# Experts of a Mamba and mixture-of-experts layer: every expert on every row, or each expert on rows sorted for it

## The chip, the cores and the metric

The kernel runs on one core of a Trainium2 chip. The metric is the device time of one execution in microseconds. The engines of the core are TensorE (PE in the profile, its weight loads PEld), VectorE (DVE), ScalarE (ACT), GpSimd (POOL) and SyncE (SP); each works through its own instructions in order and waits for the others by semaphores. SP issues most of the DMAs here.

## The reference

The input is 32 sequences of 512 tokens with 256 features, in fp32. In short form, each sequence goes through one Mamba block with an MLP, then through a mixture of experts, with layer norms between:

```python
# first part, per sequence
h = x + mamba(layernorm(x))           # inner width 512, 16 states, scan over 512 tokens
y = h + gelu(layernorm(h) @ w1.T + b1) @ w2.T + b2
x = layernorm(x + y)
# second part: 8 experts of inner width 128, two for each token, and a shared one
scores = softmax(xf @ gate_w.T)
_, idx = top_k(scores, 2)
cw = zeros(N, 8); cw[row, idx] += scores at idx
g = einsum('nd,efd->nef', xf, wg); u = einsum('nd,efd->nef', xf, wu)
y = einsum('nef,edf->ned', silu(g) * u, wd)
routed = einsum('ned,ne->nd', y, cw)
shared = silu(xf @ sg.T) * (xf @ su.T) @ sd.T
x = layernorm(x + routed + shared)
```

As written, the reference computes all eight experts for every token and multiplies six of the eight results by zero.

## The kernel before

The kernel keeps 128 channels or 128 tokens on the partitions. A sequence has four parts. `front` normalizes the tokens, projects them, applies the convolution and the gates of the time step, and stores two tables, `sdt` and `sdx`, to DRAM. `scan` runs the recurrence in 32 steps per sequence: SP loads `dtr` and `dxr` from those tables (the list `dtr<-sdt` and `dxr<-sdx`, line 322, three buffers each, two chunks of two steps ahead), `times_b` multiplies by the B table (line 357, on POOL for a quarter of the steps, else on DVE), ACT writes the decay to PSUM (line 418), DVE runs the scan instruction (line 420), POOL multiplies by the C table (line 421), and PE sums the states into `py` (line 385) two steps later. The tile `u` that goes through these steps has eight buffers. `middle` projects out, adds and runs the MLP. `back` normalizes, computes the gate's logits, routes, and runs the experts.

The parts of different sequences overlap. While `scan(b)` runs, the generator `finish(b - 1)` is advanced a unit at a time between its steps: middle of b - 1, front of b + 1, back of b - 1. The emitted order is then placed on the engines by the framework's scheduler, and each engine follows its list in order.

In `back` (lines 573 to 596) nine rounds run, for the shared expert and the eight routed ones. In each, PE computes `pg` and `pu` for the 512 tokens (line 189), ACT the tanh of the gate (line 584), DVE two operations (lines 591 and 592), PE the down projection `pd` in four pieces of 128 tokens (line 196), and DVE adds each piece to the sum `h`, scaled by the token's weight `cwt` for that expert (line 567), which is zero for six of eight. `route` (lines 482 to 524) works on small tiles of 128 x 32, mostly in PSUM. All expert weights lie in SBUF (`wg_sb`, `wu_sb`, `wd_sb`). POOL issues no DMA.

## Time and profile before

| | |
|---|---|
| median of three runs | 5848.29 us (5845.99 to 5848.46) |
| profiled execution | 5845.93 us |
| its span, first to last instruction | 5843.9 us |
| TensorE clock granted | 0.917 of full speed |
| busy: DVE, PE, POOL, ACT | 4950.2, 4875.3, 3649.2, 2965.3 us |
| DMA | 447.93 MB, mean 77 GB/s; queue of SP 22.6% of the 16 engines |

A busy time is what the instructions of one engine took together; it says nothing about what they waited for. The profile has for that the chain that ended last (from the last instruction back, each step to what released it) and, with each group of instructions, the idle time of its engine just before it and the engine that ended it. A group is one line of the code with one operation and one pair of tiles. The matmuls of fp32 appear as two passes each.

### The profile page before, as it was taken

To read this page: it belongs to the slowest core of one execution; us is meant where nothing else is said; L and a number is where in the kernel's file an instruction comes from. 1 tells how busy PE (TensorE), PEld (TensorE's weight loads), DVE (VectorE), ACT (ScalarE), POOL (GpSimd) and SP (SyncE) were. 2 spreads that over 40 slices of the span, in tenths; PEclk is the share of its full clock that TensorE was granted. 3 is DMA by queue.
4 is the path that set the end of the run, shared out by engine and by line. 5 is a ranking of instruction groups with operands and counts; after the bars stand their busy time and mean duration, and the time that the engine had idled before them with its cause. 6 is when DMAs were issued, how large, how long until landed. Compare 5 with 4: busy or idle time off the path is not lost.

```text
span 5843.9 us, 47922 instructions
## 1 busy us (share of the span) xinstructions
PE 4875.3 (83%) x14336; PEld 2073.3 (35%) x14336; DVE 4950.2 (85%) x7303; ACT 2965.3 (51%) x4512; POOL 3649.2 (62%) x2127
## 2 busy tenths in 40 slices
PE   5688888888888888888888888888888888888887
PEld 1233333333333333333333333333333333333343
DVE  6888888888889888888888888888888888888885
ACT  4544555445555445554455544455544555444542
POOL 5766666665666656666666656566666666665652
PEclk7899999999989999899998999999999999999998
DMA  4222222222221222222222212222222222222210
GB/s 149 74 78 76 75 84 75 70 83 80 73 84 64 83 78 76 82 69 78 81 73 81 85 63 82 78 72 87 69 76 76 75 84 79 68 82 80 73 58 13
DMA packets 239701, 447.93 MB, mean 77 GB/s; under 512 B 23104, under 2 KB 57024, under 8 KB 239312
## 3 DMA queue, kind: packets, MB, share of 16 engines
q1 hardware_dynamic: 236448, 439.49, 22.6%
q10 hardware_dynamic: 2992, 5.38, 0.3%
q8 instruction: 112, 1.84, 0.1%
q14 instruction: 149, 1.22, 0.1%
HBM read 358.81 MB, written 85.98 MB: 76 GB/s over the span
## 4 chain that ended last, share of the span: by engine, by line
DVE 42%; PE 36%; POOL 9%; ACT 7%; issue 4%; DMA 0%; ACTq 0%; DVEq 0%; POOLq 0%
DVE u L420 21%; PE py L385 11%; DVE u L357 6%; PE pg L189 6%; PE pd L196 6%; POOL u L421 5%; PE pu L189 4%; DVE pin L244 4%; DVE h L567 2%; PE pm L189 2%; PE pm L196 2%; ACT pda L418 2%; POOL dt L295 2%; PE pz L189 1%; POOL dtx L297 1%
## 5 line engine op out<-in xcount | busy, mean ns | idle before, releaser
L421 POOL TENSOR_TENSOR u<-u,bc 128x1024 f32<-128x1024 f32 x1024 | 2410.5, 2356 | 1778.4 <-DVE u L420 1691.1
L420 DVE TENSOR_TENSOR_SCAN u<-pda,u 128x512 f32<-128x512 f32 x2048 | 2439.5, 1211 | 121.4 <-ACT pda L418 117.3
L418 ACT ACTIVATE pda<-dtr,a_neg 128x512 f32<-128x512 f32 x2048 | 1396.7, 689 | 1338.0 <-DVE u L420 1333.3
L385 PE MATMUL py<-u,gather 128*32 128x512 f32 x4096 | 1389.1, 664 | 442.0 <-POOL u L421 393.9
L357 DVE TENSOR_TENSOR u<-dx,bc 128x1024 f32<-128x1024 f32 x768 | 923.6, 1210 | 83.2 <-ACT dx L354 78.1
L385 PEld LDWEIGHTS py<-u,gather 128*32 128x32 f32 x4096 | 238.5, 115 | 1249.6 <-POOL u L421 606.5
L189 PE MATMUL pg<-x1T,wg_sb 128*128 128x512 f32 x1152 | 634.6, 653 | 30.7 <-DVE the L591 28.1
L196 PE MATMUL pd<-wd_sb,he 128*128 128x256 f32 x2304 | 613.7, 386 | 24.6 <-DVE h L567 24.3
L357 POOL TENSOR_TENSOR u<-dxr,bc 128x1024 f32<-128x1024 f32 x256 | 602.4, 2353 | 4.8 <-PE py L385 2.8
L196 PEld LDWEIGHTS pd<-wd_sb,he 128*128 128x128 f32 x2304 | 421.0, 189 | 403.9 <-DVE h L567 168.0
L189 PE MATMUL pu<-x1T,wu_sb 128*128 128x512 f32 x1152 | 551.2, 596 | 1.3
L584 ACT ACTIVATE the<-pg 128x512 f32<-128x512 f32 x288 | 171.9, 597 | 662.9 <-PE pg L189 662.9
L567 DVE SCALAR_TENSOR_TENSOR h<-pd,cwt,h 128x256 f32<-128x256 f32 x1024 | 450.0, 480 | 55.6 <-PE pd L196 51.3
L196 PE MATMUL po<-out_sb,xc 128*128 128x256 f32 x1024 | 303.0, 452 | 53.8 <-DVE h L440 28.6
L189 PEld LDWEIGHTS pg<-x1T,wg_sb 128*128 128x128 f32 x1152 | 215.6, 206 | 281.7 <-issue 90.4
L189 PEld LDWEIGHTS pu<-x1T,wu_sb 128*128 128x128 f32 x1152 | 219.6, 193 | 269.0 <-issue 230.8
L189 PE MATMUL pin<-xnT,in_sb 128*128 128x512 f32 x512 | 252.0, 625 | 52.9 <-DVE xc L256 49.8
L244 DVE SCALAR_TENSOR_TENSOR pin<-xpad,half,pin 128x512 f32<-128x512 f32 x384 | 269.8, 748 | 22.4 <-POOL dtx L297 12.0
L196 PEld LDWEIGHTS po<-out_sb,xc 128*128 128x128 f32 x1024 | 223.8, 228 | 174.3 <-DVE xc L403 63.0
L262 PE MATMUL pdbc<-xc,xp_sb 128*48 128x512 f32 x256 | 175.0, 846 | 131.9 <-DVE xc L256 131.8
L591 DVE SCALAR_TENSOR_TENSOR the<-the,pg 128x512 f32<-128x512 f32 x288 | 195.8, 680 | 99.9 <-ACT the L584 99.9
L189 PE MATMUL pm<-hT,w_sb 128*128 128x512 f32 x512 | 239.3, 611 | 43.2 <-ACT hT L451 22.6
(107 smaller groups left out, 5030.0 us busy)
## 6 DMA issues: line engine op xcount, KB each, us to landing
dtr<-sdt SPq DMA_DIRECT2D x512, 256.0 KB, 2.9
dxr<-sdx SPq DMA_DIRECT2D x512, 256.0 KB, 3.0
bc<-rows SPq DMA_DIRECT2D x128, 512.0 KB, 4.5
sdt<-dt SPq DMA_DIRECT2D x64, 512.0 KB, 2.8
sdx<-dtx SPq DMA_DIRECT2D x64, 512.0 KB, 3.0
x<-in_x_dram SPq DMA_DIRECT2D x32, 512.0 KB, 3.8
out_dram<-h SPq DMA_DIRECT2D x32, 512.0 KB, 5.4
rows<-dbc SPq DMA_DIRECT2D x32, 64.0 KB, 1.6
```

Source lines behind the costliest of these rows:

```text
L189: nc.tensor.matmul(p, w[:, k, cols], src[:, k, :], start=(k == 0), stop=(k == KM - 1))
L196: nc.tensor.matmul(p, part[:, c * P : (c + 1) * P], w[:, j, :], start=(j == 0), stop=(j == len(parts) - 1),)
L244: nc.vector.scalar_tensor_tensor(pa, xp[:, i : i + S], half[:, w0 + i : w0 + i + 1], pa, ALU.mult, ALU.add,)
L262: nc.tensor.matmul(pd[: R + 2 * NS, :], xp_sb[:, j, :], xcs[j], start=(j == 0), stop=(j == NJ - 1),)
L357: eng.tensor_tensor(u, dx.unsqueeze(1).to_broadcast([P, GS, S]), table(0, b, g), ALU.mult)
L385: nc.tensor.matmul(py[r : r + ND, :], gather, u[:, i, :], start=False, stop=(g == NH - 1 and i == GS - 1),)
L418: nc.scalar.activation(pda, dtr, AF.Exp, scale=a_neg[:, a : a + 1])
L420: nc.vector.tensor_tensor_scan(ui, pda, ui, 0.0, ALU.mult, ALU.add)
L421: nc.gpsimd.tensor_tensor(u, u, table(1, b, g), ALU.mult)
L567: nc.vector.scalar_tensor_tensor(a, p, cw[:, c, e : e + 1], a, ALU.mult, ALU.add)
L584: nc.scalar.activation(th, pg, AF.Tanh, scale=0.5)
L591: nc.vector.scalar_tensor_tensor(th, th, 1.0, pg, ALU.add, ALU.mult)
```

## The change

Each token's row is now computed only by the two experts that it chose. The 32 sequences form groups: six of four, then four of two. For each sequence, `route` finds the two experts of each token and also, with matmuls against a triangular matrix (`before`) and ones, the token's place among the tokens of that expert in the group. `back` runs only the shared expert, and writes each token's row twice, with eight indirect DMAs from POOL, into the DRAM table `rows_in` at those places (2048 places per expert, two tables used in turn, set to zero by `clear` while sequences 0 and 1 are finished). The sum of input and shared expert goes to DRAM as `sums`.

When a group is complete, `experts(g)` computes from the counts a list of blocks of 128 rows of one expert. Their number isn't known when the program is built; it runs the worst case, 39 blocks for a group of four and 23 for a group of two. For each block SP reads two numbers from SBUF into registers and loads the block's rows and its expert's weights (a row of 768 numbers per partition) from DRAM; two blocks at a time go through transposes, gate and up projection, tanh and products, down projection, and a store to `rows_out`. At the end POOL fetches, with an indirect DMA for each 128 tokens and choice, the two result rows of each token; PE sums them, each multiplied by a diagonal matrix of the tokens' weights, and the final layer norm follows. This work is spread as a second generator, `late`, over the steps of the scans that follow.

Besides, `xpad` and `thz` have one buffer instead of two, and `dt` and `dtx` are computed in two halves. The diff, without the changes of shapes and names around it:

```diff
+    before = const.tile([P, P], F32, name="before")
+    nc.gpsimd.iota(
+        before, [[1, P]], base=0, channel_multiplier=-1, allow_small_or_imprecise_dtypes=True
+    )
+    nc.vector.tensor_scalar(before, before, 0.0, 1.0, ALU.is_gt, ALU.mult)
+    ones = const.tile([P, P], F32, name="ones")
+    nc.gpsimd.memset(ones, 1.0)
+    first = const.tile([P, E], F32, name="first")
+    for e in range(E):
+        nc.gpsimd.memset(first[:, e : e + 1], float(e * CAP))
...
-            xp = work.tile([P, NTAP - 1 + S], F32, tag="xpad", name=f"xpad_{b}_{j}")
+            xp = work.tile([P, NTAP - 1 + S], F32, tag="xpad", name=f"xpad_{b}_{j}", bufs=1)
-            th = work.tile([P, S], F32, tag="thz", name=f"thz_{b}_{j}")
+            th = work.tile([P, S], F32, tag="thz", name=f"thz_{b}_{j}", bufs=1)
...
+            dt = work.tile([P, 2, S], F32, tag="dt", name=f"dt_{b}_{j0}", bufs=1)
+            dtx = work.tile([P, 2, S], F32, tag="dtx", name=f"dtx_{b}_{j0}", bufs=1)
+            for i, j in enumerate(range(j0, j0 + 2)):
+                pa = ps.tile([P, S], F32, tag="tk", name=f"pdt_{b}_{j}")
+                nc.tensor.matmul(
+                    pa, dt_sb[:, j * P : (j + 1) * P], dbc[:R, :], start=True, stop=True
+                )
+                yield
+                nc.scalar.activation(dt[:, i, :], pa, AF.Abs, bias=col("dtb", j))
+                nc.vector.tensor_scalar(
+                    dtx[:, i, :], pa, col("dtb", j), 0.0, ALU.add, ALU.max
+                )
+            nc.scalar.activation(dt, dt, AF.Exp, scale=-1.0)
+            nc.scalar.activation(dt, dt, AF.Ln, bias=1.0)
...
+    rows_in = [scr.tile([E * CAP + P, DM], F32, name=f"rows_in{i}", bufs=1) for i in range(2)]
+    carries, slots, weights = {}, {}, {}
+
+    def clear(t):
+
+        z = work.tile([P, GS, S], F32, tag="u", name=f"zero_{t}", bufs=U_BUFS)
+        nc.gpsimd.memset(z, 0.0)
...
+        r = rows_in[t]
+        nc.sync.dma_start(
+            r[: full * P].rearrange("(m p r) d -> p m (r d)", p=P, r=n),
+            z.unsqueeze(1).to_broadcast([P, full // n, n * DM]),
+        )
...
+        nc.tensor.matmul(pos, before, both, start=True, stop=False)
+        for c in range(NC - 1):
+            k = NC - 1 - c
+            nc.tensor.matmul(
+                pos[:, c + 1 :, :],
+                ones,
+                both[:, c : c + 1, :].to_broadcast([P, k, E]),
+                start=False,
+                stop=(c == NC - 2),
+            )
+        for c in range(NC):
+            nc.tensor.matmul(tot, ones, both[:, c, :], start=(c == 0), stop=(c == NC - 1))
...
+        carry = tl("carry", [P, E])
+        nc.vector.tensor_tensor(carry, carries[g], tot, ALU.add)
+        carries[g] = carry
+        nc.vector.tensor_tensor(tmp, one, pos, ALU.mult)
+        nc.vector.tensor_reduce(slot[:, 0, :], tmp, AX.X, ALU.add)
+        nc.vector.tensor_tensor(tmp, both, pos, ALU.mult)
+        nc.vector.tensor_reduce(s2, tmp, AX.X, ALU.add)
+        nc.vector.tensor_tensor(slot[:, 1, :], s2, slot[:, 0, :], ALU.subtract)
+        idx = tl("idx", [P, TOPK * NC], I32)
+        nc.vector.tensor_copy(idx, slot.rearrange("p k c -> p (k c)"))
...
-        for e in [E, *range(E), None]:
-            if e is not None:
-                pg = ps.tile([P, S], F32, tag="mm", name=f"pg_{b}_{e}")
-                pu = ps.tile([P, S], F32, tag="mm", name=f"pu_{b}_{e}")
-                channels(pg, wg_sb[:, :, e, :], slice(0, P), x1T)
-                channels(pu, wu_sb[:, :, e, :], slice(0, P), x1T)
...
+        wg, wu, wd = parts(ws_sb)
+        channels(pg, wg, slice(0, P), x1T)
+        channels(pu, wu, slice(0, P), x1T)
+        yield
+        th = work.tile([P, S], F32, tag="th", name=f"th_{b}", bufs=1)
+        nc.scalar.activation(th, pg, AF.Tanh, scale=0.5)
+        t = work.tile([P, S], F32, tag="hid", name=f"he_{b}", bufs=HID_BUFS)
+        nc.vector.scalar_tensor_tensor(th, th, 1.0, pg, ALU.add, ALU.mult)
+        nc.vector.scalar_tensor_tensor(t, pu, 0.5, th, ALU.mult, ALU.mult)
+        r = rows_in[place[b][0] % 2]
+        for k in range(TOPK):
+            for c in range(NC):
+                i = k * NC + c
+                nc.gpsimd.indirect_dma_start(
+                    out=r,
+                    out_offset=bass.IndirectOffsetOnAxis(ap=idx[:, i : i + 1], axis=0),
+                    in_=h[:, c, :],
+                    in_offset=None,
+                    bounds_check=E * CAP + P - 1,
+                    oob_is_err=True,
+                )
+                yield
...
+            v = h[:, c0 : c0 + 2, :]
+            nc.vector.tensor_tensor(v, v, po, ALU.add)
+        sums[b] = scr.tile([P, NC, DM], F32, tag="sums", name=f"sums_{b}", bufs=3 * GROUP)
+        nc.sync.dma_start(sums[b], h)
+
+    def experts(g):
+
+        nb = n_blocks(g)
...
+        cnt, num, cum = [tl(nm, [P, E]) for nm in ("cnt", "num", "cum")]
+        nc.vector.tensor_tensor(cnt, carries.pop(g), first, ALU.subtract)
+        m = TOPK * len(groups[g]) * S // P
+        cmp = tl("cmp", [P, E * MAX_BLOCKS])
+        a = cmp[:, : E * m].rearrange("p (e m) -> p e m", m=m)
+        nc.vector.tensor_tensor(
+            a,
+            cnt.unsqueeze(2).to_broadcast([P, E, m]),
+            mults[:, :m].unsqueeze(1).to_broadcast([P, E, m]),
+            ALU.is_gt,
+        )
+        nc.vector.tensor_reduce(num, a, AX.X, ALU.add)
+        nc.vector.tensor_tensor_scan(cum, ones[:, :E], num, 0.0, ALU.mult, ALU.add)
...
+        row, wrow = [tl(nm, [P, nb], I32) for nm in ("row", "wrow")]
+        nc.vector.tensor_scalar(row, st, float(E * CAP), 1.0, ALU.min, ALU.mult)
+        nc.vector.tensor_scalar(wrow, ex, float(P), 1.0, ALU.mult, ALU.mult)
...
+        got = small.tile([P, n], I32, tag="got", name=f"got_{g}", bufs=2)
+        nc.vector.tensor_tensor(got, back_to, flat, ALU.add)
...
+        def fetch(k):
+            got = []
+            for i in range(2 * k, min(2 * k + 2, nb)):
+                r = in_order(row[0:1, i : i + 1], E * CAP)
+                x = work.tile([P, DM], F32, tag="xb", name=f"xb_{g}_{i}", bufs=4)
+                nc.sync.dma_start(x, rows_in[g % 2][bass.ds(r, P), :])
+                r = in_order(wrow[0:1, i : i + 1], E * P)
+                w = work.tile([P, NW], F32, tag="wb", name=f"wb_{g}_{i}", bufs=4)
+                nc.sync.dma_start(w, w_e[bass.ds(r, P), :])
+                got.append((x, w))
+            return got
+
+        pairs = (nb + 1) // 2
+        ahead = fetch(0)
+        for k in range(pairs):
+            pair = ahead
+            ahead = fetch(k + 1) if k + 1 < pairs else None
+            n = len(pair)
+            pt = ps.tile([P, KM, 2, P], F32, tag="tk", name=f"pt_{g}_{k}")
+            for i, (x, _) in enumerate(pair):
+                for q in range(KM):
+                    nc.tensor.transpose(pt[:, q, i, :], x[:, q * P : (q + 1) * P], ident)
...
+            xT = work.tile([P, KM, 2, P], F32, tag="xT", name=f"xT_{g}_{k}")
+            nc.scalar.copy(xT[:, :, :n, :], pt[:, :, :n, :])
...
+            pm = ps.tile([P, 2, 2, P], F32, tag="mm", name=f"pe_{g}_{k}")
+            for i, (_, w) in enumerate(pair):
+                for a, v in enumerate(parts(w)[:2]):
+                    for q in range(KM):
+                        nc.tensor.matmul(
+                            pm[:, a, i, :],
+                            v[:, q, :],
+                            xT[:, q, i, :],
+                            start=(q == 0),
+                            stop=(q == KM - 1),
+                        )
...
+            nc.scalar.activation(th_, pg, AF.Tanh, scale=0.5)
+            nc.vector.scalar_tensor_tensor(th_, th_, 1.0, pg, ALU.add, ALU.mult)
+            nc.vector.scalar_tensor_tensor(he_, pu, 0.5, th_, ALU.mult, ALU.mult)
...
+            po = ps.tile([P, 2, DM], F32, tag="tk", name=f"pd_{g}_{k}")
+            for i, (_, w) in enumerate(pair):
+                nc.tensor.matmul(
+                    po[:, i, :], he[:, i, :], parts(w)[2], start=True, stop=True
+                )
+            yb = work.tile([P, 2, DM], F32, tag="yb", name=f"yb_{g}_{k}")
+            nc.scalar.copy(yb[:, :n], po[:, :n])
+            nc.sync.dma_start(
+                rows_out[2 * k : 2 * k + n].rearrange("i p d -> p i d"), yb[:, :n]
+            )
+            yield
...
+        for i0, b in enumerate(groups[g]):
+            at = work.tile([P, NC, DM], F32, tag="at", name=f"at_{b}", bufs=1)
+            nc.sync.dma_start(at, sums.pop(b))
+            for c0 in range(0, NC, 2):
+                po = ps.tile([P, 2, DM], F32, tag="tk", name=f"pc_{b}_{c0}")
+                for c in range(c0, c0 + 2):
+                    for k in range(TOPK):
+                        i = (i0 * TOPK + k) * NC + c
+                        y = work.tile([P, DM], F32, tag="yg", name=f"yg_{b}_{k}_{c}", bufs=4)
+                        nc.gpsimd.indirect_dma_start(
+                            out=y,
+                            out_offset=None,
+                            in_=src,
+                            in_offset=bass.IndirectOffsetOnAxis(
+                                ap=got[:, i : i + 1], axis=0
+                            ),
+                            bounds_check=nb * P - 1,
+                            oob_is_err=True,
+                        )
+                        dg = work.tile([P, P], F32, tag="dg", name=f"dg_{b}_{k}_{c}", bufs=2)
+                        nc.scalar.mul(dg, ident, weights[g][:, i0, k, c : c + 1])
+                        nc.tensor.matmul(
+                            po[:, c - c0, :],
+                            dg,
+                            y,
+                            start=(k == 0),
+                            stop=(k == TOPK - 1),
+                        )
+                    yield
+                v = at[:, c0 : c0 + 2, :]
+                nc.vector.tensor_tensor(v, v, po, ALU.add)
...
+        end = min(groups[g][-1] + 2, NB) if g < len(groups) else NB
+        now = -(-n_late // max(end - b, 1))
...
+            while lately * (per - 1) < i * now and n_late:
+                next(late, None)
+                lately += 1
+                n_late -= 1
...
+        if g < len(groups) and b == groups[g][-1] + 1:
+            run(late)
+            late, n_late = experts(g), n_experts(g)
+            g += 1
...
+GROUP = 4
+CAP = GROUP * 512
+MAX_BLOCKS = TOPK * CAP // P + E - 1
-N_FINISH = 87
+N_FINISH = 70
```

## Prediction

> **What bounds the kernel now.** I read the engine shares first, then the chain that ended last, then the groups, then the stretches of one sequence. Engine shares (busy us, share of the span, instructions):
>
> ```profile
> span 5843.9 us, 47922 instructions
> PE 4875.3 (83%) x14336; PEld 2073.3 (35%) x14336; DVE 4950.2 (85%) x7303; ACT 2965.3 (51%) x4512; POOL 3649.2 (62%) x2127
> ```
>
> No engine is full: DVE and PE take turns. The chain that ended last says the same, and names the lines:
>
> ```profile
> DVE 42%; PE 36%; POOL 9%; ACT 7%; issue 4%; DMA 0%; ACTq 0%; DVEq 0%; POOLq 0%
> DVE u L420 21%; PE py L385 11%; DVE u L357 6%; PE pg L189 6%; PE pd L196 6%; POOL u L421 5%; PE pu L189 4%; DVE pin L244 4%; DVE h L567 2%; PE pm L189 2%; PE pm L196 2%; ACT pda L418 2%; POOL dt L295 2%; PE pz L189 1%; POOL dtx L297 1%
> ```
>
> The groups give durations (busy us, mean ns of one, idle before and its releaser):
>
> ```profile
> L421 POOL TENSOR_TENSOR u<-u,bc 128x1024 f32<-128x1024 f32 x1024 | 2410.5, 2356 | 1778.4 <-DVE u L420 1691.1
> L420 DVE TENSOR_TENSOR_SCAN u<-pda,u 128x512 f32<-128x512 f32 x2048 | 2439.5, 1211 | 121.4 <-ACT pda L418 117.3
> L189 PE MATMUL pg<-x1T,wg_sb 128*128 128x512 f32 x1152 | 634.6, 653 | 30.7 <-DVE the L591 28.1
> L196 PE MATMUL pd<-wd_sb,he 128*128 128x256 f32 x2304 | 613.7, 386 | 24.6 <-DVE h L567 24.3
> L189 PE MATMUL pu<-x1T,wu_sb 128*128 128x512 f32 x1152 | 551.2, 596 | 1.3
> L567 DVE SCALAR_TENSOR_TENSOR h<-pd,cwt,h 128x256 f32<-128x256 f32 x1024 | 450.0, 480 | 55.6 <-PE pd L196 51.3
> L591 DVE SCALAR_TENSOR_TENSOR the<-the,pg 128x512 f32<-128x512 f32 x288 | 195.8, 680 | 99.9 <-ACT the L584 99.9
> ```
>
> POOL waits 1691 us for the scan: today it is the servant. The stretches (length, then PE, PEld, DVE, ACT, POOL busy, clock, DMA share, GB/s), for one expert stretch, one sequence, and the tail after the last scan step:
>
> ```profile
> 2118.00:2168.00 50.00, 49.10 (x146) 22.14 (x144) 46.81 (x74) 15.67 (x25) 22.88 (x14) 1.00 0.14 47
> 2000.00:2180.00 180.00, 152.89 (x451) 64.76 (x449) 154.75 (x229) 93.02 (x142) 114.37 (x67) 0.91 0.23 77
> 5738.00:5844.00 106.00, 85.17 (x258) 48.55 (x258) 40.73 (x105) 19.66 (x32) 12.14 (x16) 0.84 0.02 5
> ```
>
> Sequences follow each other every 179.2 us (input loads from 224.8 to 5421.7 us, 29 intervals), 5.6 us for each of 32 scan steps. In the expert stretch both PE (98%) and DVE (94%) are full: the dense experts do cost time, about 50 us per sequence.
>
> **What the Trainium skill says.** "DMA: Bandwidth & Descriptors", section "Anatomy of one DMA", gives a DMA issued by GpSimd about 2.0 us plus bytes at 436 GB/s; no such DMA is in this trace, but the SP store of 64 KB lands in 1.6 us and that of 512 KB in 2.8, which agrees in size. "SBUF — State Buffer", section "SBUF: two separate sides", says that DVE and GpSimd hold one port pair exclusively: a DVE instruction with two SBUF inputs and a GpSimd instruction that reads SBUF block each other for the whole instruction. Nothing here shows it, because every large DVE operation reads one operand from PSUM.
>
> **The change part by part.** Counts after come from the order of instructions of the changed kernel.
>
> *Removed.* DVE: L567 450.0, the L565 add 50.9, eight ninths of L591 and L592 (195.8 + 196.6) = 348.8, cwt 5.8: 855 us. PE: eight ninths of 634.6 + 551.2 + 613.7 = 1600 us. ACT: eight ninths of the tanh (171.9) = 153 us.
>
> *Added on DVE.* 128 adds of 128x512 at 0.68 (L591's size) = 87; 168 pairs of blocks (326 blocks: six groups of 39, four of 23) times two operations of 128x256 at 0.48 (L567) = 161; routing, 8 small ones x 32 x 0.19 = 48; index arithmetic per group, 13 at 0.19 and 7 at some 0.45 = 5.6, x10 = 56. Sum 352, net -503: 4447 us. The last sequence is counted in the tail, so 31/32 of it, **-487 us**, taken in full because PE falls too.
>
> *Added on PE.* 652 transposes at 0.24 (48.6 to 74.4 us per 256 now) = 156; 2608 passes of 128 columns, which the trace lacks: from below the 128x8 row (69.2/512 = 0.135), from above the 128x256 row (613.7/2304 = 0.266), I take 0.19 = 496 (352 to 694); 1164 passes of 256 columns = 310; 512 small ones = 69. Net about -570 (-710 to -370).
>
> *ACT* gets two copies at 0.57 and a tanh at 0.4 per pair, 256 small diagonals at 0.3, and 42 more table loads at 1.28: net about +250, 3215 of 5850. Hidden, ACT has half its time free.
>
> *Scatters, 256 on POOL.* Each is written to the same DRAM table, so each waits for the one before to land, with all later POOL work queued behind it. Occupancy of POOL per indirect DMA: from below 1.0 us (the DMA page's first byte for software descriptors, "Latency and other measured facts"), from above 3.1 us (the SBUF page's price under port contention, "A bandwidth-pool intuition"); I take 1.5, estimated. Landing 2.0 + 131 KB/436 = 2.3. They are placed one per scan step; POOL's step is 2.36 + 0.59 for L421 and its quarter of L357, so 4.5 with a scatter, against 5.1 to 5.6 of the step. Nearly hidden; DVE's in-place sum waits for six of them to land: 2 us a sequence, **+64** (0 to 400, the latter at 3.1).
>
> *Gathers, 240 outside the tail.* The order puts the 32 of a group of four into one scan, 16 of them within three steps. The ring is four buffers: four cost 4 x 1.5 + 2.3 + 0.5 for PE = 9 us, 16 cost 36, plus three steps' own 9, against 15 of wall; 8 u buffers cover two steps, 10. Lost 20; the other 16 are spread, some 10. 30 x 6 groups and 50 for three short groups: **+230** (50 to 575). What is late: `pc` on PE, behind it `py`, then DVE's add of `at`, then the next scan step.
>
> *Index arithmetic.* About 13 operations per group have two SBUF inputs and meet POOL's 2.36 us multiplies: 0.8 each, x10, **+100** (0 to 240).
>
> *Clearing.* Two stores of 16.9 MB on SP's queue, which carries the scan's `dtr` and `dxr`. The page's 439.49 MB at 22.6% of the engines is 333 GB/s: 51 us each, 20 covered by three buffers: **+60** (0 to 150).
>
> *Fetches.* 652 register loads on SP (a floor of 0.6 us by the DMA page, same section) and 652 DMAs at 0.51 each, in order among the scan's loads; each scan load has some 20 us of lead. **+60** (0 to 300). Bytes about double to 800 MB, near 45% of the engines.
>
> *Tail.* Eight expert rounds go, -42. Added: index work 8, eight scatters with nothing to cover them 30, first fetch 6, twelve pairs one after the other (transposes 1.2, copy 0.6, 16 passes at 0.21 of the throttled tail, tanh 0.4, two DVE 1.0, down 1.0, hops 1.2: 8.8) 105, landing 3, 16 gathers 28: **+138** (90 to 200).
>
> Sum: -487 + 64 + 230 + 100 + 60 + 60 + 138 = +165 on a span of 5843.9; 2.0 us lie around the span in the profiled execution (5845.93, 2.4 below the median 5848.29). That gives 6011.
>
> **The rivals.** *The savings get through (faster).* POOL waits 1778 us before L421, so indirect DMAs at 1.0 us fit there: gathers 50, ports 30, clear and fetches 40, tail 138: -229, **5617**. It decides where four gathers take under about two scan steps. Against it: they stand in bursts. *POOL becomes the bound.* At 3.1 us POOL has 3649 + 1587 = 5240 us of work plus landings; scatters 400, gathers 575, tail 176, ports, clear and fetches 220: +884, **6730**. Against it: no large DVE operation takes both ports. *SP's queue is late:* register loads of 2 us make a pair's fetch 10 us, and 3 us of each of 168 pairs reach the scan: +500, **6510**. The slack of 20 us speaks against. That the work isn't really cut I exclude: 326 blocks stand for 1024.
>
> **How the numbers follow.** My case 0.42 (its own range 5840 to 6200), savings through 0.26, POOL bound 0.20, SP late 0.12. The range 5580 to 6700 leaves out about half of each outer case. Faster: 0.26 and 0.03 of mine; within 0.2%, about what a measurement can tell, 0.03; slower 0.68.
>
> **What would show it.** Right: DVE near 4450 and PE near 4300 us; POOL above 70%; POOL rows waiting on landings of `rows_in` and `yg`; scans that hold gathers some 30 us longer than the others; two dips in the first slices at the clears; a tail near 240 us with DVE mostly idle. Wrong: indirect DMAs that leave POOL in under 1 us, or a uniform period near 163 us; or, the other way, `dtr` loads that end the waits of `pda`, a sign of SP.

## The result, and the profile after

The changed kernel takes 6304.69 us, the median of four runs (6298.69 to 6308.18), against 5847.8 us before (5845.99 to 5848.46). The ratio is 1.0781, with a 95% interval of 1.0762 to 1.0799: 457 us slower, where the forecast said some 163 slower (6011 us). The side was right and the time lies in the forecast's range, but the loss is nearly three times as large.

The page of the changed kernel: span, and busy time, share and instructions of each engine.

```profile
span 6301.6 us, 56782 instructions
PE 4452.6 (71%) x15176; PEld 2096.6 (33%) x15176; DVE 4537.7 (72%) x6548; ACT 3215.7 (51%) x5122; POOL 4185.4 (66%) x2652
```

The work did go (L802 and L819 below stand for the dense L189 and L196): DVE fell by 412 us and PE by 423. Yet the span grew, so DVE stands idle for 1764 us, where it was 894. The clock granted to TensorE fell too, from 0.917 of full speed to 0.824, but that alone doesn't make the kernel slow: a run below has 0.817 and takes 5233 us. The chain that ended last covers only a fifth of the span and names no engine (shares by engine; a q marks the engine's own sequencer):

```profile
PE 6%; POOL 5%; DVE 4%; issue 3%; DMA 2%; ACT 1%; SPq 0%; POOLq 0%; ACTq 0%; DVEq 0%
```

The groups (busy us, mean ns of one, idle of the engine before them, its releaser):

```profile
L448 POOL TENSOR_TENSOR u<-u,bc 128x1024 f32<-128x1024 f32 x1024 | 2406.4, 2354 | 882.2 <-DVE u L447 528.5
L447 DVE TENSOR_TENSOR_SCAN u<-pda,u 128x512 f32<-128x512 f32 x2048 | 2430.0, 1207 | 287.9 <-ACT pda L445 270.0
...
L802 PE MATMUL pe<-xT,wb 128*128 128x128 f32 x2608 | 387.0, 309 | 31.6 <-ACT xT L796 27.3
L819 PE MATMUL pd<-wb,hb 128*128 128x256 f32 x652 | 213.0, 453 | 116.9 <-DVE xc L283 46.5
...
L670 POOL DMA_INDIRECT rows_in<-h,idx x256 | 265.0, 1035 | 235.5 <-DMA rows_in<-h,idx 114.5
L839 POOL DMA_INDIRECT yg<-rows_out,got x256 | 266.6, 1042 | 224.1 <-DMA rows_out<-yb 105.8
L685 DVE TENSOR_TENSOR h<-h,ps 128x512 f32<-128x512 f32 x64 | 43.7, 682 | 191.3 <-DMA rows_in<-h,idx 191.3
```

POOL's waits for the scan fell from 1691 to 529 us, but it is no bound at 66%. An indirect DMA keeps POOL for 1.03 us only. But DVE waits 191 us in front of line 685, the add in place of the shared expert into `h`. The view of waits has a second one, which the forecast did not have, for the input of the sequence after the next (us in total, times, longest):

```profile
DVE h L685 <- DMA rows_in<-h,idx: 191.3, 49, 17.7
DVE st_a L186 <- DMA x<-in_x_dram: 132.2, 26, 12.9
```

In the kernel before, the waits for the load of `x` were 7.8 us in all.

The stretches (length, then PE, PEld, DVE, ACT, POOL busy, clock, DMA share, GB/s) of an early scan before any expert block runs, of a scan with gathers, and of what follows the start of the last scan:

```profile
728.00:906.00 178.00, 112.60 (x336) 44.59 (x336) 131.99 (x179) 88.04 (x132) 120.88 (x71) 0.82 0.25 83
2207.00:2412.00 205.00, 141.73 (x425) 60.12 (x424) 143.91 (x221) 107.23 (x181) 161.07 (x116) 0.84 0.35 114
5864.00:6302.00 438.00, 275.23 (x1084) 166.41 (x1080) 178.84 (x352) 139.83 (x248) 172.31 (x135) 0.76 0.38 117
```

The first row is the surprise. Nothing of the late part runs there, DVE has 132 us of work and PE 113, and still the scan takes 178 us, as long as before with its dense rounds. The forecast's savings of 487 us over 31 scans would make it 163, with the late part's work for DVE already in it. From one first scan instruction to the next, taken from the trace, in us:

```
before         133 177 178 180 178 180 178 180 ...                   last: 266 to the end
after          122 176 182 178 178 199 175 186 205 175 176 186 205
               ... 208 200 196 219 210 179 207                       last: 438 to the end
```

So three things are to be explained: the base that didn't fall, the longer scans of the late part (205 us where the gathers stand; the last seven are long throughout), and an end that is 172 us longer, counted from the start of the last scan, for which the kernel before had this stretch:

```profile
5578.00:5844.00 266.00, 218.69 (x658) 106.44 (x658) 176.88 (x303) 90.78 (x142) 109.27 (x67) 0.88 0.09 31
```

### The profile page after: what moved, and what is told of

The parts are those of the page before. It is cut to its first block, busy times and chain, and to the rows that moved or that the text cites. A ratio compares the mean times of both kernels' runs of the same rounds, so it can differ in the third digit from the quotient of the medians.

```text
span 6301.6 us, 56782 instructions
## 1 busy us (share of the span) xinstructions
PE 4452.6 (71%) x15176; PEld 2096.6 (33%) x15176; DVE 4537.7 (72%) x6548; ACT 3215.7 (51%) x5122; POOL 4185.4 (66%) x2652
## 5 line engine op out<-in xcount | busy, mean ns | idle before, releaser
L670 POOL DMA_INDIRECT rows_in<-h,idx x256 | 265.0, 1035 | 235.5 <-DMA rows_in<-h,idx 114.5
L839 POOL DMA_INDIRECT yg<-rows_out,got x256 | 266.6, 1042 | 224.1 <-DMA rows_out<-yb 105.8
L802 PE MATMUL pe<-xT,wb 128*128 128x128 f32 x2608 | 387.0, 309 | 31.6 <-ACT xT L796 27.3
L802 PEld LDWEIGHTS pe<-xT,wb 128*128 128x128 f32 x2608 | 365.2, 221 | 109.3 <-ACT xT L796 68.2
L381 ACT COPY dx<-dxr 128x512 f32<-128x512 f32 x384 | 225.1, 586 | 171.6 <-DVE u L384 163.7
L819 PE MATMUL pd<-wb,hb 128*128 128x256 f32 x652 | 213.0, 453 | 116.9 <-DVE xc L283 46.5
L216 PE MATMUL pz<-xnT,in_sb 128*128 128x512 f32 x512 | 253.7, 613 | 1.5 <-DVE th L664 1.0
L851 PE MATMUL pc<-yg,dg 128*128 128x256 f32 x512 | 188.1, 490 | 80.2 <-DMA yg<-rows_out,got 53.0
L223 PE MATMUL pm<-w_sb,hid 128*128 128x256 f32 x1024 | 238.4, 387 | 6.2 <-ACT hid L498 6.1
L223 PEld LDWEIGHTS pm<-w_sb,hid 128*128 128x128 f32 x1024 | 195.9, 194 | 49.2 <-issue 12.4
```

Of the source, the lines that this page charges most:

```text
L216: nc.tensor.matmul(p, w[:, k, cols], src[:, k, :], start=(k == 0), stop=(k == KM - 1))
L223: nc.tensor.matmul(p, part[:, c * P : (c + 1) * P], w[:, j, :], start=(j == 0), stop=(j == len(parts) - 1),)
L381: nc.scalar.copy(dxps[kc], dxrs[kc])
L670: nc.gpsimd.indirect_dma_start(out=r, out_offset=bass.IndirectOffsetOnAxis(ap=idx[:, i : i + 1], axis=0), in_=h[:, c, :], in_offset=None, ...
L802: nc.tensor.matmul(pm[:, a, i, :], v[:, q, :], xT[:, q, i, :], start=(q == 0), stop=(q == KM - 1),)
L839: nc.gpsimd.indirect_dma_start(out=y, out_offset=None, in_=src, in_offset=bass.IndirectOffsetOnAxis(ap=got[:, i : i + 1], axis=0), bounds_ ...
```

## The experiments

**Room and dense work.** Theory 1 was that a sequence's `finish` is a chain and that the scatters lengthen it; theory 2, that the edits which make room slow `front`; theory 3, that `x` comes late by its place in the order.

Only the room (`xpad` and `thz` with one buffer, `dt` in halves) in the kernel before:

```diff
-            th = work.tile([P, S], F32, tag="thz", name=f"thz_{b}_{j}")
+            th = work.tile([P, S], F32, tag="thz", name=f"thz_{b}_{j}", bufs=1)
```

> The kernel before with only the edits that make room: one buffer each for xpad and thz, dt and dtx in halves. Theory 1 (the sequence's own finish is a serial chain through the one buffer of h, and routing plus eight scatters took the place of the dense rounds in it) says these edits cost little: 5850, at most 5910. Theory 2 (the room-making edits slowed the front of each sequence, and so held the period at 178 us instead of the 163 us forecast) says about 15 us for each of 31 sequences, so 6200 to 6350. Theory 3 (the x load comes late in the changed order) says 5850.

5833.95 us, ratio 0.9978 (0.9969 to 0.9986): slightly faster. Theory 2 falls; the run without scatters below has these edits too, and there the scans follow each other every 161.5 us.

Only the dense routed rounds taken from the kernel before:

```diff
-        for e in [E, *range(E), None]:
+        for e in [E, None]:
...
-N_FINISH = 87
+N_FINISH = 63
```

> The kernel before without the eight routed expert rounds; it leaves the routed experts out and keeps the shared one, the routing and all else. If the 487 us of the forecast were there to be had once the routed rounds go, it takes 5300 to 5400 (period about 163 us). If the period is set by something that the dense rounds do not lengthen, it stays at 5700 to 5850. Theory 1 (chain of the finish) says that the chain gets some 50 us shorter and the period falls at least to 163 us: 5150 to 5400.

5219.88 us, ratio 0.8927 (0.8909 to 0.8945), 160.4 us from scan to scan: more was to be had than the 5300 to 5400 that stand for the forecast's 487 us. It is no full return, though. DVE's busy time falls by 744 us here (4950.2 to 4206.1) and the time by 627, some 84% of it.

**Scatters and late part apart.** The changed kernel without its late part:

```diff
-        sums[b] = scr.tile([P, NC, DM], F32, tag="sums", name=f"sums_{b}", bufs=3 * GROUP)
-        nc.sync.dma_start(sums[b], h)
+        nc.sync.dma_start(out[b].rearrange("(c p) d -> p c d", p=P), h)
...
-            late, n_late = experts(g), n_experts(g)
+            late, n_late = iter(()), 0
...
-        run(experts(g))
```

> The changed kernel without its late part: no blocks, no weight fetches, no gathers, no last layer norm (the sum with the shared expert is stored straight to the output); clears, routing and scatters stay. Theory 1 (routing and scatters in the finish hold the period) says that the period stays near 176 us in all sequences: 5650 to 5800, and PE and DVE wait on the landings of the scatters or on h. If instead the late work fills the engines and sets the period, it falls to about 150 us a sequence: 4900 to 5100.

5876.99 us, 180.8 us from scan to scan, nearly all alike: as slow as the kernel before, with neither dense rounds nor blocks, and slower than theory 1 had it. The same without the scatters and clears:

```diff
-                nc.gpsimd.indirect_dma_start(
-                    out=r,
...
-        if b < 2:
-            clear(b)
```

> The run without the late part, and without the eight scatters and the two clears either; the routing to the slot numbers stays, and the sum with the shared expert goes to the output. Theory 1 says that h comes free some 30 us earlier in each sequence and the period falls to 145 to 155 us: 4750 to 5050, some 750 us below the run that keeps the scatters. Theory 2 and theory 3 (room-making edits; x load late by its place in the order) say no fall beyond the clears: within 100 us of the run that keeps the scatters.

5233.43 us, 161.5 from scan to scan, again above theory 1's range. The difference is of the size that it gave (some 750): scatters and clears cost 644 us here, 19.3 per scan. One sequence of each run, with scatters and without (columns as above):

```profile
2899.60:3083.40 183.80, 120.84 (x336) 46.83 (x336) 131.43 (x179) 87.79 (x132) 120.52 (x71) 0.77 0.24 81
```

```profile
2603.70:2764.10 160.40, 116.54 (x338) 44.51 (x336) 130.96 (x178) 88.70 (x134) 112.18 (x63) 0.82 0.26 86
```

POOL has 8 us more to do, eight scatters, and DVE nothing: this scan is 23 us longer by waiting. The waits of the run with scatters say where:

```profile
DVE st_a L186 <- DMA x<-in_x_dram: 362.6, 31, 13.2
DVE h L685 <- DMA rows_in<-h,idx: 204.7, 34, 18.4
PE po L223 <- DVE h L685: 100.6, 31, 19.8
```

The two DVE rows make 567 us, and of the first only 6.4 are left without scatters; that is most of the 644. The chain, with its times after the first scan instruction of one sequence in this run: `idx`, the places of the rows, at 20 us, eight scatters from 20 to 52, the second add of line 685 at 55, store at 56, first add of the next `middle` (line 467) at 62, and POOL's add of `x` (line 484) at 78. Only that add frees the buffer of `x`, and the load of `x`, for the sequence two on, is issued right after it. From the timeline (start, length, group, idle before), with other lines between these:

```profile
2954.36 0.68 DVE L685 TENSOR_TENSOR h<-h,ps 128x512 f32<-128x512 f32 x1
2961.67 0.73 DVE L467 TENSOR_TENSOR h<-x,po 128x256 f32<-128x256 f32 x2
2977.43 2.35 POOL L484 TENSOR_TENSOR h<-h,x 128x1024 f32<-128x1024 f32 x1 [2.64 <-ACT nrmB L195]
2979.80 0.38 SPq L234 DMA_DIRECT2D x<-in_x_dram  x1
2983.79 0.75 DVE L186 BATCH_NORM_STATS2 st_a<-x 128x6 f32<-128x256 f32 x2 [12.72 <-DMA x<-in_x_dram]
```

Without scatters line 467 stands at 8 us and line 484 at 25, in a scan that starts at 2443.1 us:

```profile
2451.10 0.74 DVE L467 TENSOR_TENSOR h<-x,po 128x256 f32<-128x256 f32 x2
2468.53 2.35 POOL L484 TENSOR_TENSOR h<-h,x 128x1024 f32<-128x1024 f32 x1 [2.32 <-ACT nrmB L195]
```

Theory 3 saw the right wait, but it is the end of the chain and no fault of the order alone.

**What holds the chain.** 1a: the one buffer of `h`. 1b: each scatter waits for the landing of the one before, as they write one table.

```diff
-        h = work.tile([P, NC, DM], F32, tag="h", name=f"h_{b}", bufs=1)
+        h = work.tile([P, NC, DM], F32, tag="h", name=f"h_{b}", bufs=2)
```

> The run without the late part (scatters and clears kept), with two buffers of h instead of one. Theory 1a: the 36 us from idx to the store of the sum count because h has one buffer, so the next sequence's middle can't start. Then two buffers bring the period from 181 us to about 161 to 165: 5240 to 5400. Theory 1b: POOL's own list is held, because each scatter waits for the landing of the one before it on the same table with the scan's multiplications queued behind it. Then two buffers change little: 5800 to 5880.

5703.91 us: 173 won, neither number. Now eight tables and one buffer of `h`:

```diff
-        r = rows_in[place[b][0] % 2]
...
+                r = own[i]
```

> The run without the late part (scatters and clears kept), one buffer of h, but each of the eight scatters writes a table of its own, so that none waits for the one before it to land; the rows thus lie in eight tables and nothing reads them. Theory 1b (POOL held by landings): 5240 to 5400. Theory 1a (one buffer of h): the sum still comes after eight scatters placed a step apart, so only a few us a sequence are won, 5700 to 5880.

5369.69 us, 163.9 from scan to scan: 507 won of 644. 1b is the larger part, though not as stated: POOL waits 48 us for landings in all. Its timeline in the changed kernel (start, length, group, idle before):

```profile
745.00 1.12 POOL L670 DMA_INDIRECT rows_in<-h,idx  x1 [0.32 <-DVE idx L624]
746.16 2.35 POOL L448 TENSOR_TENSOR u<-u,bc 128x1024 f32<-128x1024 f32 x1
748.68 1.02 POOL L670 DMA_INDIRECT rows_in<-h,idx  x1 [0.17 <-issue]
749.73 2.35 POOL L448 TENSOR_TENSOR u<-u,bc 128x1024 f32<-128x1024 f32 x1
752.25 1.02 POOL L670 DMA_INDIRECT rows_in<-h,idx  x1 [0.17 <-PE py L412]
753.31 2.35 POOL L384 TENSOR_TENSOR u<-dxr,bc 128x1024 f32<-128x1024 f32 x1
755.61 2.35 POOL L448 TENSOR_TENSOR u<-u,bc 128x1024 f32<-128x1024 f32 x1
758.12 1.02 POOL L670 DMA_INDIRECT rows_in<-h,idx  x1 [0.17 <-issue]
```

and in the run with eight tables:

```profile
2856.62 1.13 POOL L671 DMA_INDIRECT own<-h,idx  x1 [0.32 <-DVE idx L625]
2858.05 0.97 POOL L671 DMA_INDIRECT own<-h,idx  x1 [0.30 <-issue]
2859.33 0.97 POOL L671 DMA_INDIRECT own<-h,idx  x1 [0.30 <-issue]
2860.61 0.97 POOL L671 DMA_INDIRECT own<-h,idx  x1 [0.30 <-issue]
```

With one table there are one or two multiplications between two scatters, 3.6 to 5.9 us from one to the next, in which the landing (2.5 us) is hidden; with eight tables they follow every 1.28 us. The eight take 30 us or 9. POOL itself loses little by either. What is late is the add that stands behind them.

The other part of the chain is that this add works in place. With two buffers of `h` it still holds the two PSUM buffers `tk` until the scatters have landed, and the next `middle` needs one (PE waits for line 685 above). So the sum gets a tile of its own:

```diff
-            v = h[:, c0 : c0 + 2, :]
-            nc.vector.tensor_tensor(v, v, po, ALU.add)
+            v = work.tile([P, 2, DM], F32, tag="th", name=f"sum_{b}_{c0}", bufs=1)
+            nc.vector.tensor_tensor(v, h[:, c0 : c0 + 2, :], po, ALU.add)
```

> The run without the late part (scatters and clears kept, all on one table), with two buffers of h, and with the sum with the shared expert written to a tile of its own instead of in place, so that neither h nor the two PSUM buffers tk wait for the scatters to land. Theory 1c: what holds the next sequence's middle is the pair of tk buffers and h, both behind an add in place that waits for landings. Then 161 to 167 us a sequence: 5240 to 5430, with the eight scatters still some 4 us apart. Theory 1b (POOL's list itself is held by the landings, wherever the sum goes): 5650 to 5710, as with two buffers of h alone.

5472.56 us, 231 below the run with two buffers of `h`. The scatters are still 3 to 6 us apart, and now no other engine waits for them (POOL does, for 145 us in all): line 467 is back at 8 us, and DVE's wait for `x` falls to 21.1 us. 1c holds, though the run is 43 us above its range's top and 103 above the run with eight tables.

**In the whole kernel.** Two buffers of `h` alone:

```diff
-        h = work.tile([P, NC, DM], F32, tag="h", name=f"h_{b}", bufs=1)
+        h = work.tile([P, NC, DM], F32, tag="h", name=f"h_{b}", bufs=2)
...
-            xT = work.tile([P, KM, 2, P], F32, tag="xT", name=f"xT_{g}_{k}")
+            xT = work.tile([P, KM, 2, P], F32, tag="xT", name=f"xT_{g}_{k}", bufs=1)
...
-            yb = work.tile([P, 2, DM], F32, tag="yb", name=f"yb_{g}_{k}")
+            yb = work.tile([P, 2, DM], F32, tag="yb", name=f"yb_{g}_{k}", bufs=1)
```

> The whole changed kernel with two buffers of h; the room comes from xT and yb, which have one instead of two. Theory 1a says that the scatters' 19.3 us for each of some 31 sequences come back in full, while gathers and tail stay: 5680 to 5760, below the kernel before. Theory 1b says 6250 to 6310. If one buffer of xT and yb slows the pairs of blocks, it shows in the scans that hold them and in the tail, and adds up to 100.

6282.47 us, ratio 1.0744 (1.0726 to 1.0762): 22 us, as 1b had it. What the single buffers of `xT` and `yb` cost in it was not separated. Then the sum apart as well, stored to `sums` by halves:

```diff
+            nc.sync.dma_start(sums[b][:, c0 : c0 + 2, :], v)
```

> The whole changed kernel with two buffers of h (room from xT and yb, one each) and the sum written to a tile of its own. Theory 1c, in full: the base period falls from 178 to about 165 us in the 30 scans, some 400 us, so 5850 to 5950; gathers, short groups and tail stay. If the scans that hold pairs and gathers are bound by these and not by the chain, only 100 to 200 come back: 6080 to 6180. Theory 1b: 6250 to 6290.

6044.59 us, ratio 1.0346 (1.0328 to 1.0363): 260 won, between the two cases. In place of both, eight tables, with `r = own[i]` as above:

> The whole changed kernel with each of the eight scatters of a sequence writing a table of its own, so that none waits for the landing of the one before; the blocks still read the common table, which holds only the zeros of the clearing, so the routed experts are left out of the output while all work is done. Without the late part this edit was worth 507 us. If the waits of one scatter for the other are the term that the forecast missed, and the rest of its sum holds, 5800 to 5900; if the late part fills what they leave, as in the version with the sum apart (6044.6), 5950 to 6050.

6074.05 us, ratio 1.0386 (1.0365 to 1.0407): 231 won, where the same edit without the late part won 507, and above both ranges of the expectation. The costs don't add up, so the fourth corner of the table was run, the changed kernel without its scatters:

```diff
-                nc.gpsimd.indirect_dma_start(
-                    out=r,
-                    out_offset=bass.IndirectOffsetOnAxis(ap=idx[:, i : i + 1], axis=0),
-                    in_=h[:, c, :],
...
```

> The whole changed kernel without its 256 scatters, so that the rows never reach the table and the blocks work on its zeros; clears, routing, fetches, pairs, gathers and tail stay. It completes a table of four: neither scatters nor late part 5233.4 (without the clears), scatters alone 5877.0, both 6304.7. If the two costs add up, 5233 + 428 and some 30 for the clears: 5660 to 5720. If the late part fills the time that the scatters leave, as the version with the sum apart says (572 us for it) and the one with eight tables (704 us): 5800 to 5960.

5960.34 us, ratio 1.0193 (1.0163 to 1.0222): slower than before even so, at the top of the second range. (The blocks multiply zeros here; PE is busy for 4432 us, where it was 4453.)

| us | without scatters | with scatters | scatters cost |
|---|---|---|---|
| without late part | 5233 (no clears) | 5877 | 644 (with the clears) |
| with late part | 5960 | 6305 | 344 |
| late part costs | 727 | 428 | |

In the whole kernel, the two waits of DVE account for most of the 344: 191.3 + 132.2 = 323.5 us with scatters, 19.6 without. DVE's busy time hardly differs (4538 and 4540 us); its idle time is 347 us longer. The clears are in the 727: the second to fourth intervals are 179, 173, 163 us where the run without them has 152, 161, 161, so some 41 us. Without the late part the scatters alone thus cost about 600 us, an estimate by subtraction.

**Inside the late part.** Without the gathers, in the changed kernel:

```diff
-                        nc.gpsimd.indirect_dma_start(
-                            out=y,
...
                             dg,
-                            y,
+                            at[:, c, :],
```

> The changed kernel without the 256 gathers: the sum takes the rows of at where the fetched rows stood, so the result of the routed experts is left out of the output, and all blocks are still computed. The forecast's terms say that gathers cost 230 us in the scans and 28 in the tail: about 6045. If the short groups' 148 us and the 172 us of the tail are mostly gathers, 5900 to 6000; if they are mostly pairs, 6100 to 6150.

6122.08 us: the gathers cost 183 us, as in the case that the rest is mostly pairs. The scan that holds a group's gathers falls from 204.5 to 186.8 us, so they make 18 us of it. Without the pairs of blocks, in the version with the sum apart:

```diff
-        pairs = (nb + 1) // 2
-        ahead = fetch(0)
-        for k in range(pairs):
...
-        src = rows_out.rearrange("i p d -> (i p) d")
+        src = rows_in[g % 2]
```

> The version with two buffers of h and the sum in a tile of its own (6044.6 us), without the 168 pairs of blocks: no fetches, no products, no rows_out; the gathers read rows_in instead, so the routed experts' result is left out. Without any late part this version takes 5472.6, so the whole late part costs 572 us here. If gathers and index work make up most of it: 5850 to 5950. If the pairs fill the engines: 5600 to 5750, and the gather scans fall from 212 us to about 190.

5803.06 us: pairs and fetches cost 241, gathers, index work and the rest 331. Its intervals show where (after the first six):

```
with pairs      158 169 211 170 159 169 215 170 ...  220 208 170 208   last: 406
without pairs   184 174 175 175 184 174 175 175 ...  174 184 178 173   last: 298
```

The time lies between the two cases. Four scans in the middle take some 710 us either way, some 10 us a scan over the 167 of the run without a late part; the difference lies in the last seven scans, 199.9 against 179.6 us (142 in all), and after them, 108. That doesn't show that the pairs are free in the middle, nor what makes the scan of 211 us, which is gone without pairs (184 at most). The edit moves the gathers too, as the pairs' units leave `n_experts` with them: in the trace, 11, 9, 12 and 0 of a group's 32 stand in its four scans, where with pairs all 32 stand in the last of the four. Pairs and places of gathers are not separated by this run.

Other group sizes and other spacing of the gathers, in the same version:

```diff
-    while NB - sum(sizes) > 2 * GROUP:
+    while NB - sum(sizes) > GROUP:
```

> The same version (6044.6 us) with seven groups of four and two of two instead of six and four: 319 blocks instead of 326, and the short groups' extra work in three scans instead of seven. The scans from 24 on take 199.9 us against 175.6 for those before them. If the short groups with their seven blocks of padding are the cost, 30 to 100 us come back: 5945 to 6015. If what costs is that the work of the last sequences is pressed into the last scans, the same work in fewer scans wins nothing: 6035 to 6100.

6006.02 us, ratio 1.0274 (1.0257 to 1.0291): 39 won, as in the first case: the last seven scans (187.1 each) save 89, what follows takes 46 of it back.

```diff
-                    yield
+                        yield
+                        yield
```

> The same version (6044.6 us) with the gathers spread: two units of the late generator after each two gathers of a token row, 17 units a sequence in place of 5, so that the 32 gathers of a group of four go over about half of its four scans instead of one. If the gather scan's 212 us (159 to 170 in the others) come from the burst against four buffers of yg, 20 to 30 us a group come back: 5850 to 5950. If a gather costs the same wherever it stands, the mean of the four scans stays at 175: 6020 to 6070.

(with 17 in place of 5 units a sequence in `n_experts`.) 6162.8 us, ratio 1.0533 (1.0507 to 1.056): 118 lost, against both cases; 21 and 11 of a group's gathers stand in two scans now.

> Both edits of the two runs before it together, the other group sizes and the spread gathers. If each wins what its first case says: 5770 to 5900, near or below the kernel before; if neither does, 6020 to 6100.

6113.87 us, ratio 1.0459 (1.0441 to 1.0476), outside both cases: the other sizes win 49 us on the spread gathers, but the spread loses 108 on the other sizes. Then the gathers denser, with the other sizes:

```diff
-                    yield
                 v = at[:, c0 : c0 + 2, :]
                 nc.vector.tensor_tensor(v, v, po, ALU.add)
+                yield
```

> The version with two buffers of h, the sum apart and seven groups of four (6006.0 us), with the gathers made denser: one unit of the late generator after four gathers, three units a sequence in place of five. Spreading them cost 118 us. If what a gather costs is the time in which its sum holds one of the two tk buffers in PSUM, denser gathers win: 5900 to 5980. If the burst against four buffers of yg costs as much, 5990 to 6040.

6245.94 us, ratio 1.0674 (1.0656 to 1.0692): 240 lost against the run with the other sizes alone, and again outside both cases. Spread and denser both lose, which neither the hold of `tk` nor the burst explains alone. Each also shifts the pairs against the scan steps, as the units of the late part are handed out evenly (8, 10, 2 and 0 pairs in a group's four scans with the gathers spread, 6, 6, 7 and 1 without); that wasn't separated, and what sets the price of a gather's place stays open.

**A version that beats both, by 1%.** The chain pointed back to the dense kernel, whose `h` has one buffer too: the kernel before with the room, and two buffers of `h`:

```diff
-        h = work.tile([P, NC, DM], F32, tag="h", name=f"h_{b}", bufs=1)
+        h = work.tile([P, NC, DM], F32, tag="h", name=f"h_{b}", bufs=2)
```

> The dense kernel (the kernel before with the edits that make room) with two buffers of h. If the single buffer of h was what set the period of 179 us in the kernel before too, its period falls towards the 155 us of DVE's and PE's work: 5200 to 5500. If the dense rounds themselves fill PE and DVE, as the forecast took it, it stays within 60 us of 5834.

5790.43 us, ratio 0.9903 (0.9886 to 0.9919), 177.5 us from scan to scan. This is the fastest kernel here that leaves nothing out, 57 us below the kernel before, of which 13 are the room's. The base hardly moves, so in the dense kernel the rounds themselves set the period, as the forecast had it. No routed version came below the kernel before.

## Why the prediction was right or wrong

*The sum, by its terms.* The tail here is what follows the last scan instruction, as in the forecast: 106.1 us before, 61.1 without scatters and late part, 226.3 with the late part alone, 258.4 with both. The measured column goes one way through the table above: 5848 to 5233 to 5960 to 6305.

| us | forecast | measured |
|---|---|---|
| dense rounds out, routing and shared adds in, over the scans | (855 - 44 - 48) x 31/32 = -739 | -614 + 45 = -569 |
| late part, over the scans | 252 + 450 = +702 | 727 - 165 = +562 |
| scatters, over the scans | +64 | 344 - 32 = +312 |
| tail | +138 | +152 |
| sum | +165 | +457 |

The dense rounds gave 170 us less than forecast and the late part cost 140 less. That these nearly cancel is luck. What remains is the scatters' term, 248 us too small in an error of 292. The split depends on the way through the table, but put in before the late part the scatters cost more still, about 600 us.

*The step that failed* is "They are placed one per scan step ... Nearly hidden; DVE's in-place sum waits for six of them to land: 2 us a sequence, **+64**". The placing was right, and so was the landing (2.5 us for 2.3). An indirect DMA held POOL for 1.03 us, the lower end of the estimate and not the 1.5 taken. But the step priced POOL's time and one wait, not the length of the chain. The sum waits 191.3 / 32 = 6.0 us a sequence instead of 2, and the step stopped at the sum. Late next are `tk` and `h`, the next `middle`, POOL's add, and the load of `x`, for which DVE stops again: some 10 us a sequence together. Undoing the wait in one place (eight tables) or the holding (sum apart, two buffers of `h`) gave 231 and 260 us back in the whole kernel. The 312 lie in the term's own range of 0 to 400 by luck, as its upper end stood for indirect DMAs of 3.1 us.

*Savings of 487 "taken in full because PE falls too".* Only in part. Without scatters and late part, DVE's busy time fell by 757 us, as the terms say (763), and the time by 614, about four fifths. In the changed kernel even that is hidden by the chain. The forecast's own sign of error, "a uniform period near 163", was the picture without scatters.

*Rivals.* "POOL becomes the bound" is refuted: it is 66% busy, and no indirect DMA holds it for over 1.3 us. The forecast had POOL above 70% among the signs of being right, so that sign failed with the 1.5 us. "SP's queue is late" is refuted by the sign that the prediction gave for it: ACT waits 33.0 us in all for `dtr`, nearly all in one wait of 32.8 us, and the run without the late part has that wait too (33.1). In it the load stands on SP's list behind the store of `sums`, which waits 51.1 us for the sum of line 685: beside the second clear the scatters landed after up to 7.2 us instead of 2.5. So where SP was late once, the chain of the scatters made it so, not the fetches. The 652 register loads took SP 0.27 us each, not the 0.6 taken as a floor. "The savings get through" needed indirect DMAs at 1.0 us; they were at 1.0 us, and the savings still did not get through, because the point of decision lay in the chain and not on POOL.

*Gathers, 230 and 28 in the tail.* Measured 183, of which 20 in the tail, where 32 stand and not 16. A group of four loses 25 us by them over its four scans, for 30 said. *Tail, +138.* Measured +152; the scatters are 32 of it, for 30 said. *Clears, +60.* About 41. The store of 16384 KB landed in 44.3 us, for 51 worked out. *Short groups, 50 for their gathers.* The last seven scans take 202.6 us against 185.6 for the eighteen before them, 119 more, and still 194.4 against 180.2 without any gather, 99 more. The forecast had no term for these 99. The trace has 44 pairs in six of these scans, where 20 stand in four before, so the blocks pressed into them are the likely cause.

*Busy times.* DVE 4537.7 for 4450 and PE 4452.6 for 4300, both forecasts a little low; ACT 3215.7 for 3215. The tail is 258 us for 240 said, with DVE busy for 46 of them.

*Index arithmetic, 56 + 100.* The lines 698 to 750 take 115 us of DVE, of which 49 are above the fastest of each kind. The rows of one small add show what the forecast took from the Trainium skill, "SBUF — State Buffer", section "SBUF: two separate sides", that a DVE operation with two SBUF inputs and one of GpSimd that reads SBUF exclude each other:

```profile
L733 DVE TENSOR_TENSOR cum<-cum,num 128x8 f32<-128x8 f32 x10 | 16.6, 1662 | 0.0
```

The mean of 1.66 us hides two kinds. In seven of the ten a multiplication of POOL runs at the same time; they take 2.1 to 2.7 us and end within 0.04 us of it. In three none runs, and they take 0.15 us, with an indirect DMA on POOL beside them or without. One of each from the timeline, with POOL:

```profile
930.67 2.33 POOL L448 TENSOR_TENSOR u<-u,bc 128x1024 f32<-128x1024 f32 x1 [0.91 <-DVE u L447]
930.80 2.23 DVE L733 TENSOR_TENSOR cum<-cum,num 128x8 f32<-128x8 f32 x1
...
5072.58 0.15 DVE L733 TENSOR_TENSOR cum<-cum,num 128x8 f32<-128x8 f32 x1
5072.66 1.04 POOL L839 DMA_INDIRECT yg<-rows_out,got  x1 [0.16 <-issue]
```

The trace agrees that the two exclude each other. The page gives the ports to the one that starts first; two of the seven began 0.13 and 0.28 us before the multiplication and still ended behind it, and nothing here shows why.

## What to carry to other kernels

A DMA that reads a tile holds what is written over it later, and everything that holds: for each new DMA write down who may touch its source next, which buffers that one keeps meanwhile, and which load starts when they come free. Writes to one DRAM table were a queue in effect here (eight took 30 us, and 9 with tables of their own), though POOL was seen to wait for landings for only 48 us in all; tables of their own, or a result out of place, take the waits out of the chain. And costs along one chain hide each other: about 600 us alone were 344 beside the late part, so a term is measured in the kernel where it will stand.

## What the runs showed of the hardware

An indirect DMA on POOL that writes 128 rows of 1 KB to DRAM took POOL 1.03 us and landed after 2.5 us; one that fetches 128 such rows took 1.04 and landed after 2.9. Eight independent ones followed each other every 1.28 us. A store of 16384 KB from one SBUF tile took 44.3 us, 379 GB/s; beside it, scatters landed after up to 7.2 us, and a load of the scan issued right behind the first of the two after 43.9. An add on DVE of 128x8 with two SBUF inputs took 0.15 us in three of ten cases, and 2.1 to 2.7 us in the seven beside a multiplication on POOL; an indirect DMA on POOL did not delay it. A register load on SP from SBUF took 0.27 us.
